# A convolution and GRU kernel: the first inputs loaded as rows and turned by TensorE, the first convolution on 32x32 tiles

## The chip, the cores and the metric

The kernel runs on one core of one Trainium2 chip. A core has five engines that run side by side and wait for one another by semaphores: TensorE (PE, matrix products, with its weight loads shown as PEld), VectorE (DVE), ScalarE (ACT), GpSimd (POOL) and SyncE (SP). 16 DMA engines move data between the chip's memory (HBM) and the core's memory (SBUF, 128 partitions); products land in PSUM. The metric is the device time of one execution in microseconds (us). The kernel before takes 1041.6 us (median of 3 runs, 1041.51 to 1042.34).

## The reference

The input x is 16 sequences of 256 steps with 512 channels, cond is 16 x 512, all in float32. First comes a causal convolution over time, separate for each channel, with 16 taps, and cond is its weights (its row k is tap k). Its result is added to x. The sum feeds a GRU cell step by step over the 256 steps, with cond as the first state too (its row b is the state of sequence b). The result is the sum plus the GRU's states.

```
x = x + conv(x, cond[:, None, :])                 # y[t] = sum_k cond[k] * x[t - 15 + k]
gi = x_t @ W_ih + b_ih ;  gh = h @ W_hh + b_hh     # 512 -> 3 x 512: r, z, n
r = sigmoid(i_r + h_r);  z = sigmoid(i_z + h_z)
n = tanh(i_n + r * h_n); h = (1 - z) * n + z * h
out = x + h
```

W_ih and W_hh are 512 x 1536, 3 MB each.

## The kernel before

**Layout.** A channel's place is (q, partition): the 512 channels lie as 4 groups q of 128 partitions, and a group's partition 32j + l is channel 128j + 32q + l. With that order a 32x32 block transpose on VectorE carries a tile with (j, sequence) on its partitions over to one with channels on its partitions. Time goes in 16 chunks of 16 steps (`CHUNKS`); a chunk's columns are 16 steps x 16 sequences = 256. `xT[c]` holds a chunk of x by channels, with a halo of 15 x 16 = 240 columns of the chunk before it; `x1T[c]` holds x plus its convolution.

**The loads.** `load_x` (L119) brings a chunk as 8 DMAs of 64 KB with rows of 512 bytes, 16 sequences by 8 steps by 128 channels each, into `x_nat`, shared out over the queues of SP, ScalarE and GpSimd for the first two chunks. cond comes in four small DMAs (L140) into `cond_nat`. `load_weights` (L171) brings a gate's weights in four DMAs (L173), on SP's queue and GpSimd's, in the order W_ih for n, W_ih for r and z, then W_hh for r, n and z, all issued in the program in front of the loop; biases are between (L158 to L163). Each queue's DMAs start in its engine's order. A DMA waits for an earlier one on the same kind of queue when its semaphore is used again, eight further on.

**The order** is written by hand: every engine executes its instructions in the order in which the program emits them (`manual_schedule`).

- `mark` and `idle_products(PAD)` (L540): four products on zeros, then 108 products of one column that compute nothing of use, and a drain, after which TensorE waits.
- `prepare_cond` (L191): VectorE turns cond to `condT` and makes `last1`, the last tap plus one (x itself is added with it).
- `turn_units(0)` (L212): VectorE turns chunk 0 in two transposes of 512 columns (L222).
- Chunk 0's convolution is split. Groups q = 0, 1 are on VectorE: one product with `last1` each (L554), then 15 taps each (L265; tap k touches 16(k+1) columns). Groups q = 2, 3 (`Q_PE`) are on TensorE: `conv_on_tensor` (L278) lets ScalarE make 32 diagonal 128x128 matrices, the identity scaled by a tap (L288), and multiplies x by each (L292), summing in PSUM; ScalarE evicts the two results (L300).
- The turns of chunk 1 (again L222) stand between VectorE's taps of chunk 0; ScalarE copies the halo (L218) and computes the first term of chunk 1's four groups (L239), between the two evictions.
- `spread_biases` (L362), seeds of the PSUM tiles by ScalarE (L371, L374), the n part of x1 @ W_ih for 8 steps (`pni`, L320, evicted at L332), the r and z part for two steps (`prz`, L383).
- `bulk.run(0, HEAD)` (L601) gives VectorE the next 27 taps of chunk 1, and step 0 five more.

**The loop** (L606) calls `step` (L403) 256 times: recurrent products for r (into `prz`), n (into `pnh`) and z on L418, 32 rows of the trace each (a float32 product is two passes), and after them, on TensorE, the input products of later steps. ScalarE and VectorE make r (L435), `rn` (L447), its transpose (L449), n (L451, tanh L459), z (L461, L465) and the new state `hist` by a scan (L474). `seen` (L398) is a one-element copy with which VectorE waits for ScalarE; step 0's stands on VectorE behind the 32 taps of chunk 1. Step 0 multiplies `condT` as the state, so it needs all of W_hh. Step 1's r products wait for step 0's `hist`.

Of the kernel before, what the change touches and what calls it, by code (L numbers as in the profile page):

```python
# [24 lines left out]
F32 = mybir.dt.float32  # L25
BF16 = mybir.dt.bfloat16
AF = mybir.ActivationFunctionType
ALU = mybir.AluOpType
PSUM = bass.MemoryType.PSUM

P = 128
L = 32
GT = 8
R, Z, N = 0, 1, 2
CHUNKS = (16,) * 16
PAD = 108
HEAD = 11.0
SYNC = mybir.DependencyInfo(mybir.DependencyClass.Sync, mybir.DependencyReason.DATA)
Q_PE = (2, 3)
NI = 8  # L40
# [35 lines left out]
def conv_gru_kernel(  # L76
# [21 lines left out]
    starts = [sum(CHUNKS[:c]) for c in range(NCH)]  # L98

    const = ctx.enter_context(tc.tile_pool(name="const", bufs=1))  # L100
# [5 lines left out]
    op = ctx.enter_context(tc.tile_pool(name="op", bufs=3))  # L106
    dram = ctx.enter_context(tc.tile_pool(name="dram", bufs=1, space=bass.MemoryType.DRAM))
    ps = ctx.enter_context(tc.tile_pool(name="ps", bufs=1, space=PSUM))
    ps_ni = ctx.enter_context(tc.tile_pool(name="ps_ni", bufs=2, space=PSUM))

    ctx.enter_context(tc.manual_schedule())

    def by_part(natural):
        return natural.rearrange("p (q l) -> p q l", q=NQ)
# [4 lines left out]
    def load_x(c, queues=((nc.sync,), (nc.sync,)), behind=None):  # L119

        n = CHUNKS[c]
        t = xin.tile([P, max(CHUNKS) // 2, P], F32, tag="x_nat", name=f"x_nat_{c}")
        for s in range(2):
            for j in range(NQ):
                made = queues[s][j % len(queues[s])].dma_start(  # L125
                    out=t[32 * j + B * s : 32 * j + B * s + B, 0 : n // 2],
                    in_=x[:, starts[c] + s : starts[c] + n : 2, j * P : (j + 1) * P],
                )
                if s == j == 0 and behind is not None:
                    tc.add_manual_dep(made.ins, behind.ins.name, SYNC, reason="later in time")  # L130
        x_nat[c] = t

    cond_nat = const.tile([P, P], F32)
    nc.vector.memset(cond_nat, 0.0)

    warm = const.tile([P, 1], F32)
    nc.vector.memset(warm, 0.0)
    blank = const.tile([P, 2 * P], BF16)
    nc.vector.memset(blank, 0.0)
    for j in range(NQ):  # L140
        (nc.sync, nc.scalar)[j % 2].dma_start(
            out=cond_nat[32 * j : 32 * j + B, :], in_=cond[:, j * P : (j + 1) * P]
        )
    load_x(0, ((nc.sync, nc.scalar), (nc.gpsimd,)))
    nc.scalar.activation(warm, warm, AF.Sigmoid)
    ident = const.tile([P, P], F32)
    make_identity(nc, ident)


    b_two = const.tile([2, 3 * C], F32)  # L150
# [3 lines left out]
    bn_nat = const.tile([P, P], F32)  # L154
    nc.vector.memset(bn_nat, 0.0)

    load_x(1, ((nc.sync,), (nc.gpsimd,)))
    nc.sync.dma_start(out=b_two[0:1, :], in_=b_hh.rearrange("(o c) -> o c", o=1))  # L158
    nc.sync.dma_start(
        out=b_two[1:2, 0 : 2 * C], in_=b_ih[0 : 2 * C].rearrange("(o c) -> o c", o=1)  # L160
    )
    nc.gpsimd.dma_start(
        out=bn_nat[0:P:L, :], in_=b_ih[2 * C : 3 * C].rearrange("(j c) -> j c", j=NQ)  # L163
    )


    wih_rz = const.tile([P, NQ, 2 * C], F32)
    wih_n = const.tile([P, NQ, C], F32)
    whh = [const.tile([P, NQ, C], F32, name=f"whh_{g}") for g in range(3)]

    def load_weights(w_sb, w, g, queues):  # L171
        for j in (0, 2, 1, 3):
            queues[j].dma_start(  # L173
                out=w_sb[L * j : L * j + L],
                in_=w[j * P : (j + 1) * P, g * C : g * C + w_sb.shape[2]].rearrange(
                    "(q l) c -> l q c", l=L
                ),
            )


    for tile_of, g in ((wih_n, N), (wih_rz, R)):
        load_weights(tile_of, w_ih, g, (nc.sync, nc.sync, nc.gpsimd, nc.gpsimd))
    zero_z = [const.tile([P, NQ * B * 2], F32, name=f"zero_z_{i}") for i in range(2)]
    for t in zero_z:
        nc.gpsimd.memset(t, 0.0)


    condT = const.tile([P, NQ, L], F32)
    last1 = const.tile([P, NQ], F32)

    def prepare_cond():  # L191
        nc.vector.transpose(condT, by_part(cond_nat))
        nc.vector.tensor_scalar_add(last1, condT[:, :, K - 1], 1.0)

    bnT = const.tile([P, NQ, L], F32)

# [3 lines left out]
    xT, x1T, ni = {}, {}, {}  # L200
# [3 lines left out]
    evictions = []  # L204
# [7 lines left out]
    def turn_units(c):  # L212

        def halo():
            xT[c] = xtp.tile([P, NQ, HALO + CMAX], F32, tag="xT", name=f"xT_{c}")
            if c:
                m = CHUNKS[c - 1] * B
                nc.scalar.copy(xT[c][:, :, 0:HALO], xT[c - 1][:, :, m : m + HALO])  # L218

        def turn(a):  # L220
            o = HALO + a * PAIR
            nc.vector.transpose(  # L222
                xT[c][:, :, o : o + GT * B].rearrange("p q (a r) -> p a q r", r=L),
                x_nat[c][:, a : a + GP].rearrange("p a (q l) -> p a q l", q=NQ),
            )
            if 2 * (a + GP) == CHUNKS[c] and 4 < c + 3 < NCH:
                load_x(c + 3)

        return [(0.0, halo)] + [
            (0.7, lambda a=a: turn(a)) for a in range(0, CHUNKS[c] // 2, GP)  # L230
        ]

    def first_terms(c):

        x1T[c] = x1p.tile([P, NQ, CMAX], F32, tag="x1T", name=f"x1T_{c}")
        n = CHUNKS[c] * B

        def first(q):
            nc.scalar.activation(  # L239
                x1T[c][:, q, 0:n],  # L240
                xT[c][:, q, HALO : HALO + n],
                AF.Copy,
                scale=last1[:, q : q + 1],
            )

        for q in range(NQ):
            firsts.append((c, q, lambda q=q: first(q)))

    def give_firsts(most=99):
        for _ in range(min(most, len(firsts))):  # L250
            firsts.pop(0)[2]()

    def lag(k):

        return (K - 1 - k) * B
# [19 lines left out]
            (0.135 + n / 960.0, lambda k=k, q=q: tap(k, q)) for k in range(K - 1) for q in range(NQ)  # L275
        ]

    def conv_on_tensor():  # L278

        n = CHUNKS[0] * B  # L280
        diag = const.tile([P, len(Q_PE), K, P], F32)

        def weight(k, q):
            return condT[:, q, k : k + 1] if k < K - 1 else last1[:, q : q + 1]

        for i, q in enumerate(Q_PE):
            for k in reversed(range(K)):
                nc.scalar.activation(diag[:, i, k], ident, AF.Copy, scale=weight(k, q))  # L288
        for i, q in enumerate(Q_PE):
            acc = ps_ni.tile([P, CHUNKS[0] * B], F32, tag="pni", name=f"conv_{q}")  # L290
            for k in reversed(range(K)):
                nc.tensor.matmul(  # L292
                    acc[:, lag(k) : n],
                    lhsT=diag[:, i, k],
                    rhs=xT[0][:, q, HALO : k * B + n],
                    start=(k == K - 1),
                    stop=(k == 0),
                    skip_group_check=True,
                )
            evictions.append(lambda q=q, acc=acc: nc.scalar.copy(x1T[0][:, q, 0:n], acc[:, 0:n]))  # L300


    blocks = [(t0, NI) for t0 in range(0, T, NI)]
# [235 lines left out]
    bulk = Plan()  # L539
    mark()  # L540
    idle_products(PAD)
    nc.tensor.drain()
    (_, halo), *turns = turn_units(0)
    halo()
    for t in hist:
        nc.vector.memset(t[:, 0:L], 0.0)
    prepare_cond()
    for _, fn in turns:
        fn()
    first_terms(0)  # L550
    firsts.clear()
    for q in range(NQ):
        if q not in Q_PE:
# [2 lines left out]
                xT[0][:, q, HALO : HALO + CHUNKS[0] * B],  # L556
                last1[:, q : q + 1],
            )
    conv_on_tensor()

    taps = [fn for i, (_, fn) in reversed(list(enumerate(tap_units(0)))) if i % NQ not in Q_PE]
    needed = (NI - 1) * (NQ - len(Q_PE))
    for fn in taps[:needed]:
        fn()
    for _, fn in turn_units(1):
        fn()
    nc.vector.transpose(bnT, by_part(bn_nat))
    for fn in taps[needed:]:
        fn()
    evictions.pop(0)()  # L570
    first_terms(1)
    give_firsts()
    evictions.pop(0)()
    spread_biases()
    nc.scalar.copy(b_rows, spare)
    seed_rz(0)
# [14 lines left out]
    for c in range(1, NCH):  # L591
        due = starts[c] - NI
        taps = tap_units(c)
# [4 lines left out]
        at = len(taps) - AHEAD  # L598
# [1 line left out]
            bulk.add(cost, due, fn)  # L600
    bulk.run(0, HEAD)  # L601

    h = (lambda kc: condT[:, kc, 0:B], condT[:, :, 0:B])
    late = []
    of_pair, of_block = [], []
    for t in range(T):  # L606
        p, s = divmod(t, 2)
# [23 lines left out]
        h = step(t, h, bulk_work, other_products)  # L631
# [41 lines left out]
```

## Time and profile before

| What | us |
|---|---|
| median of 3 runs (lowest, highest) | 1041.6 (1041.51, 1042.34) |
| the profiled execution, first to last instruction (the span) | 1039.8 |
| TensorE busy | 1022.6 (98%) |
| VectorE busy | 926.8 (89%) |
| ScalarE busy | 380.3 (37%) |
| GpSimd busy | 12.4 (1%) |
| step 1's first recurrent product starts | 36.33 |

The page prints the span alone; the profiled execution's own time has what lies around it on top, and the median run is 1.8 us above the span. In the lines of the profile, a timeline row starts with its start and its length in us, then the engine, the line of the program, the operation, the tile written and the tile read, their shapes, how many were merged into the row, and in brackets how long the engine was idle before it and what ended that. A row of the chain of waits has start, length and what the time went to; "issue" is time in which an engine waited for nothing that the profile shows. A row of the busy times by stretches has the stretch and its length, then the busy time and number of instructions of TensorE, its weight loads, VectorE, ScalarE and GpSimd, and last the granted clock, the share of the 16 DMA engines and GB/s.

### The profile page before, as it was taken

Reading aid. Unit: us, or ns where it says so; the run is one execution under the profiler, and the core shown is the slowest. Engines: PE = TensorE matmul, PEld = TensorE weight load, DVE = VectorE, ACT = ScalarE, POOL = GpSimd, SP = SyncE. Lnnn points to the kernel's source line nnn. Section 1 sums busy time; section 2 is a strip of 40 time slices with the busy share of each in tenths; the row PEclk is TensorE's granted clock in tenths of the full one; section 3 lists DMA queues with packets and bytes.
Section 4 is the critical chain, followed back from the end, with each engine's and each line's share of the span. In section 5 each row is a group of like instructions: output and inputs, shape, how many; then the busy total and the mean of one; then the engine's idle time right before and its main releaser. Section 6 shows DMA issues by size and latency. Waiting matters only on the chain.

```text
span 1039.8 us, 71852 instructions
## 1 busy us (share of the span) xinstructions
PE 1022.6 (98%) x32952; PEld 928.5 (89%) x32952; DVE 926.8 (89%) x3606; ACT 380.3 (37%) x1520; POOL 12.4 (1%) x29
## 2 busy tenths in 40 slices
PE   7899999999999999999999999999999999999997
PEld 6699999999999999999999999999999999999986
DVE  7899999999999999999999999999999999896555
ACT  6233433334333333433334333343433334333332
POOL 4000000000000000000000000000000000000000
PEclk9999999999999999999999999999999999999999
DMA  9420101101010010100100010010000000000000
GB/s 216 111 58 13 26 15 29 21 15 31 8 35 14 15 35 8 32 15 19 30 14 26 14 34 15 15 34 5 15 14 15 15 13 6 15 15 15 14 11 17
DMA packets 40850, 27.72 MB, mean 27 GB/s; under 512 B 6686, under 2 KB 38498, under 8 KB 40548
## 3 DMA queue, kind: packets, MB, share of 16 engines
q1 hardware_dynamic: 38756, 18.78, 8.0%
q8 instruction: 257, 4.21, 1.7%
q0 software_dynamic: 1376, 4.20, 1.7%
q14 instruction: 45, 0.37, 0.1%
q10 hardware_dynamic: 416, 0.16, 0.1%
HBM read 14.73 MB, written 8.39 MB: 22 GB/s over the span
## 4 chain that ended last, share of the span: by engine, by line
PE 95%; DMA 3%; DVE 1%; SPq 0%; issue 0%; ACT 0%; DVEq 0%; ACTq 0%
PE prz L418 42%; PE pnh L418 21%; PE prz L383 20%; PE pni L320 10%; DMA whh<-in_L_cond_W_hh_dram 2%; DMA x_nat<-in_x_dram 1%; DVE rnT L449 0%; DVE zp L461 0%; DVE rn L447 0%; SPq L125 0%; ACT zero_z L465 0%; DVE n L451 0%; DMA out_dram<-o 0%; DVE hist L474 0%; DVE glance L398 0%
## 5 line engine op out<-in xcount | busy, mean ns | idle before, releaser
L418 PE MATMUL prz<-whh,hist 128*32 128x128 f32 x16320 | 539.9, 273 | 3.0 <-DVE hist L474 2.1
L418 PEld LDWEIGHTS prz<-whh,hist 128*32 128x32 f32 x16320 | 450.0, 103 | 8.5 <-DVE hist L474 6.6
L265 DVE SCALAR_TENSOR_TENSOR x1T<-xT,condT,x1T 128x256 f32<-128x256 f32 (+2 forms) x930 | 377.4, 462 | 0.0
L418 PE MATMUL pnh<-whh,hist 128*32 128x128 f32 x8160 | 269.7, 273 | 0.0
L383 PE MATMUL prz<-wih_rz,x1T 128*32 128x256 f32 x4096 | 268.2, 379 | 0.1
L418 PEld LDWEIGHTS pnh<-whh,hist 128*32 128x32 f32 x8160 | 226.7, 104 | 0.0
L459 ACT ACTIVATE dn<-n 128x64 f32<-128x64 f32 x256 | 67.9, 265 | 325.9 <-DVE n L451 325.9
L383 PEld LDWEIGHTS prz<-wih_rz,x1T 128*32 128x32 f32 x4096 | 129.0, 110 | 43.7 <-issue 0.3
L320 PEld LDWEIGHTS pni<-x1T,wih_n 128*32 128x32 f32 x4096 | 122.8, 110 | 42.7 <-ACT x1T L300 0.6
L435 ACT ACTIVATE r<-prz 128x128 f32<-128x128 f32 x256 | 71.1, 278 | 238.6 <-PE prz L418 235.5
L320 PE MATMUL pni<-x1T,wih_n 128*32 128x128 f32 x4096 | 158.1, 273 | 0.0
L474 DVE TENSOR_TENSOR_SCAN hist<-zero_z,dn 128x32 f32<-128x32 f32 (+1 forms) x768 | 128.6, 216 | 0.0
L447 DVE TENSOR_TENSOR rn<-r,pnh 128x128 f32<-128x128 f32 x256 | 72.4, 283 | 38.5 <-PE pnh L418 37.2
L465 ACT ACTIVATE zero_z<-zp 128x32 f32<-128x32 f32 x512 | 90.6, 226 | 8.6 <-DVE zp L461 1.8
L449 DVE STREAM_TRANSPOSE rnT<-rn 128x128 f32<-128x128 f32 x256 | 79.7, 311 | 8.7
L461 DVE STREAM_TRANSPOSE zp<-prz 128x128 f32<-128x128 f32 x256 | 80.9, 316 | 1.8 <-PE prz L418 1.7
L332 ACT ACTIVATE ni<-pni,bnT 128x128 f32<-128x128 f32 x128 | 47.1, 368 | 74.7 <-PE pni L320 74.7
L467 DVE TENSOR_TENSOR dn<-hist,dn 128x64 f32<-128x64 f32 x255 | 58.4, 229 | 11.3
L451 DVE TENSOR_TENSOR n<-rnT,ni 128x64 f32<-128x64 f32 x256 | 57.7, 225 | 8.9
L398 DVE COPY glance<-r 1x1 f32<-1x1 f32 x256 | 34.0, 133 | 25.3 <-ACT r L435 25.3
L371 ACT COPY prz<-b_rows 128x256 f32<-128x256 f32 x128 | 48.5, 379 | 0.0
L398 DVE COPY glance<-zero_z 1x1 f32<-1x1 f32 x256 | 36.3, 142 | 8.0 <-ACT zero_z L465 0.3
(51 smaller groups left out, 211.1 us busy)
## 6 DMA issues: line engine op xcount, KB each, us to landing
out_dram<-o SPq DMA_DIRECT2D x248, 32.0 KB, 1.7
x_nat<-in_x_dram SPq DMA_DIRECT2D x118, 64.0 KB, 3.0
whh<-in_L_cond_W_hh_dram POOLq DMA_DIRECT2D x8, 256.0 KB, 14.7
wih_rz<-in_L_cond_W_ih_dram POOLq DMA_DIRECT2D x2, 512.0 KB, 10.2
wih_rz<-in_L_cond_W_ih_dram SPq DMA_DIRECT2D x2, 512.0 KB, 14.3
whh<-in_L_cond_W_hh_dram SPq DMA_DIRECT2D x4, 256.0 KB, 19.0
x_nat<-in_x_dram POOLq DMA_DIRECT2D x8, 64.0 KB, 5.4
wih_n<-in_L_cond_W_ih_dram POOLq DMA_DIRECT2D x2, 256.0 KB, 7.7
```

The source lines that it names most:

```text
L265: nc.vector.scalar_tensor_tensor(out=x1T[c][:, q, to], in0=xT[c][:, q, k * B + to.start : k * B + n], scalar=condT[:, q, k : k + 1], in1=x ...
L320: nc.tensor.matmul(hold[q][32 * j : 32 * j + 32, 0:n], lhsT=wih_n[:, kc, j * P + q * L : j * P + q * L + L], rhs=x1T[c][:, kc, o : o + n], ...
L383: nc.tensor.matmul(rz[p % 2][32 * j : 32 * j + 32], lhsT=x1T[c][:, kc, o : o + PAIR], rhs=w_rz[:, :, j * P : (j + 1) * P], start=False, st ...
L398: nc.vector.tensor_copy(glances[i][0:1], of_scalar[0:1, 0:1])
L418: product = nc.tensor.matmul(dst[32 * j : 32 * j + m], lhsT=h[0](kc), rhs=whh[g][:, kc, j * P : (j + 1) * P], start=False, stop=(kc == NQ ...
L435: of_r = nc.scalar.activation(r, pr, AF.Sigmoid)
L447: nc.vector.tensor_mul(rn, r, pnh)
L449: nc.vector.transpose(rnT, by_part(rn))
L459: nc.scalar.activation(dn_v[:, :, :, 1], n, AF.Tanh)
L461: nc.vector.transpose(zp, by_part(pz))
L465: nc.scalar.activation(z_v[:, qs, :, 1], zp[:, qs, half], AF.Sigmoid) for qs in halves
L474: nc.vector.tensor_tensor_scan(hist_g[:, lo + at : lo + end], z[:, to], dn[:, to], 0.0, op0=ALU.mult, op1=ALU.add,)
```

## The change

The first two chunks of x and cond are loaded in another shape and turned by another engine, the diagonal matrices are smaller and made by other engines, and several parts of the head stand in another order.

- `load_rows` loads half a chunk (8 steps x 16 sequences = 128 rows of 2 KB) as one DMA of 256 KB, on SP's queue or ScalarE's; four of these replace 16 loads. cond is one DMA with 16 rows of 2 KB.
- `turn_by_tensor` multiplies 16 blocks of 32 channels with an identity, which transposes them into a PSUM tile (the pool `turning` has one). VectorE copies chunk 0's two halves to `xT[0]`, ScalarE chunk 1's two to `xT[1]`. `condT` has 16 columns for each group instead of 32.
- The diagonals are 128 x 32: a 32x32 diagonal on each 32 partitions. VectorE sums the identity into this form (`ident_l`), and `make_diag` multiplies it by all taps of a group at once, on VectorE for q = 2 and on GpSimd for q = 3. `conv_on_tensor(q)` has four 32x32 products for each tap.
- The order: 72 idle products and no drain; behind them cond's turn on TensorE, then chunk 0's two halves, the convolution of q = 2, chunk 1's first half, the convolution of q = 3, chunk 1's second half. On ScalarE both evictions and then the first terms of chunk 1 follow the copies of chunk 1's halves. VectorE does all 30 taps of chunk 0 in one go. On GpSimd the diagonal and the zeroing of `zero_z` stand in front of the load of `bn_nat` and the weights. On SP the weights follow the biases as before, with two x loads in front instead of six.

```diff
-PAD = 108
+PAD = 72
+    turning = ctx.enter_context(tc.tile_pool(name="turning", bufs=1, space=PSUM))
...
+    def load_rows(c, half, queue):
+        t = const.tile([P, C], F32, name=f"x_rows_{c}_{half}")
+        t0 = starts[c] + half * GT
+        queue.dma_start(
+            out=t, in_=x[:, t0 : t0 + GT, :].rearrange("b t c -> t b c")
+        )
+        x_rows[c, half] = t
...
-    load_x(0, ((nc.sync, nc.scalar), (nc.gpsimd,)))
+    nc.scalar.dma_start(out=cond_nat, in_=cond)
+    for c in range(2):
+        for half in range(2):
+            load_rows(c, half, (nc.sync, nc.scalar)[half])
...
+    nc.vector.tensor_reduce(
+        out=ident_l,
+        in_=ident.rearrange("p (i l) -> p l i", l=L),
+        op=ALU.add,
+        axis=mybir.AxisListType.X,
+    )
...
-    load_x(1, ((nc.sync,), (nc.gpsimd,)))
...
+    def turn_by_tensor(turned, rows, unit):
+        for q in range(NQ):
+            for j in range(NQ):
+                at = j * P + q * L
+                nc.tensor.matmul(
+                    turned[L * j : L * j + L, q],
+                    lhsT=rows[:, at : at + L],
+                    rhs=unit,
+                    start=q == 0,
+                    stop=q == NQ - 1,
+                    skip_group_check=True,
+                )
...
-        nc.vector.transpose(condT, by_part(cond_nat))
+        turned = turning.tile([P, NQ, K], F32, tag="turned", name="cond_turned")
+        turn_by_tensor(turned, cond_nat, ident[0:B, 0:B])
+        nc.vector.tensor_copy(condT, turned)
...
+    def turn_rows(c, half, engine):
+        turned = turning.tile([P, NQ, P], F32, tag="turned", name=f"x_turned_{c}_{half}")
+        turn_by_tensor(turned, x_rows[c, half], ident)
+        to = xT[c][:, :, HALO + half * P : HALO + half * P + P]
+        if engine is nc.scalar:
+            nc.scalar.copy(to, turned)
+        else:
+            engine.tensor_copy(to, turned)
...
+    def make_diag(engine, q):
+        diag[q] = const.tile([P, K, L], F32, name=f"diag_{q}")
+        parts = ((slice(0, K - 1), condT[:, q, 0 : K - 1]), (slice(K - 1, K), last1[:, q : q + 1]))
+        for to, w in parts:
+            n = to.stop - to.start
+            engine.tensor_tensor(
+                out=diag[q][:, to],
+                in0=ident_l.unsqueeze(1).broadcast_to([P, n, L]),
+                in1=w.unsqueeze(2).broadcast_to([P, n, L]),
+                op=ALU.mult,
+            )
...
-        for i, q in enumerate(Q_PE):
-            for k in reversed(range(K)):
-                nc.scalar.activation(diag[:, i, k], ident, AF.Copy, scale=weight(k, q))
...
+        for k in reversed(range(K)):
+            for j in range(NQ):
+                rows = slice(L * j, L * j + L)
                 nc.tensor.matmul(
-                    acc[:, lag(k) : n],
-                    lhsT=diag[:, i, k],
-                    rhs=xT[0][:, q, HALO : k * B + n],
+                    acc[rows, lag(k) : n],
+                    lhsT=diag[q][rows, k],
+                    rhs=xT[0][rows, q, HALO : k * B + n],
...
-    nc.tensor.drain()
...
     prepare_cond()
-    for _, fn in turns:
-        fn()
+    make_diag(nc.vector, Q_PE[0])
+    for q in Q_PE[1:]:
+        make_diag(nc.gpsimd, q)
+    nc.gpsimd.dma_start(
+        out=bn_nat[0:P:L, :], in_=b_ih[2 * C : 3 * C].rearrange("(j c) -> j c", j=NQ)
+    )
+    for tile_of, g in ((wih_n, N), (wih_rz, R)):
+        load_weights(tile_of, w_ih, g, (nc.sync, nc.sync, nc.gpsimd, nc.gpsimd))
+    turn_units(0)[0][1]()
+    turn_rows(0, 0, nc.vector)
+    turn_rows(0, 1, nc.vector)
...
-    conv_on_tensor()
+    conv_on_tensor(Q_PE[0])
+    turn_units(1)[0][1]()
+    turn_rows(1, 0, nc.scalar)
+    for q in Q_PE[1:]:
+        if len(evictions) > 1:
+            evictions.pop(0)()
+        conv_on_tensor(q)
+        if q == Q_PE[1]:
+            turn_rows(1, 1, nc.scalar)
...
-    evictions.pop(0)()
     first_terms(1)
+    while evictions:
+        evictions.pop(0)()
     give_firsts()
-    evictions.pop(0)()
...
-    h = (lambda kc: condT[:, kc, 0:B], condT[:, :, 0:B])
+    h = (lambda kc: condT[:, kc], condT)
```

More of the change, by code (lines that the diff above doesn't have):

```diff
@@ L131, in load_x @@
         x_nat[c] = t
-    cond_nat = const.tile([P, P], F32)
-    nc.vector.memset(cond_nat, 0.0)
+    def load_rows(c, half, queue):
[5 more added lines that the diff above has]
+        x_rows[c, half] = t
+    x_rows = {}
+    cond_nat = const.tile([B, C], F32)
     warm = const.tile([P, 1], F32)
@@ L139, in conv_gru_kernel @@
     nc.vector.memset(blank, 0.0)
[L140 to L143, printed above, removed]
-    load_x(0, ((nc.sync, nc.scalar), (nc.gpsimd,)))
+    nc.scalar.dma_start(out=cond_nat, in_=cond)
+    for c in range(2):
+        for half in range(2):
+            load_rows(c, half, (nc.sync, nc.scalar)[half])
     nc.scalar.activation(warm, warm, AF.Sigmoid)
@@ L147, in conv_gru_kernel @@
     make_identity(nc, ident)
+    ident_l = const.tile([P, L], F32)
+    nc.vector.tensor_reduce(
[4 more added lines that the diff above has]
+    )
     b_two = const.tile([2, 3 * C], F32)
@@ L160, in conv_gru_kernel @@
         out=b_two[1:2, 0 : 2 * C], in_=b_ih[0 : 2 * C].rearrange("(o c) -> o c", o=1)
-    )
-    nc.gpsimd.dma_start(
-        out=bn_nat[0:P:L, :], in_=b_ih[2 * C : 3 * C].rearrange("(j c) -> j c", j=NQ)
     )
@@ L178, in load_weights @@
             )
-    for tile_of, g in ((wih_n, N), (wih_rz, R)):
-        load_weights(tile_of, w_ih, g, (nc.sync, nc.sync, nc.gpsimd, nc.gpsimd))
     zero_z = [const.tile([P, NQ * B * 2], F32, name=f"zero_z_{i}") for i in range(2)]
@@ L185, in conv_gru_kernel @@
         nc.gpsimd.memset(t, 0.0)
-    condT = const.tile([P, NQ, L], F32)
+    condT = const.tile([P, NQ, K], F32)
     last1 = const.tile([P, NQ], F32)
+    def turn_by_tensor(turned, rows, unit):
[10 more added lines that the diff above has]
+                )
     def prepare_cond():
-        nc.vector.transpose(condT, by_part(cond_nat))
+        turned = turning.tile([P, NQ, K], F32, tag="turned", name="cond_turned")
+        turn_by_tensor(turned, cond_nat, ident[0:B, 0:B])
+        nc.vector.tensor_copy(condT, turned)
         nc.vector.tensor_scalar_add(last1, condT[:, :, K - 1], 1.0)
+    def turn_rows(c, half, engine):
[6 more added lines that the diff above has]
+            engine.tensor_copy(to, turned)
     bnT = const.tile([P, NQ, L], F32)
@@ L276, in tap_units, with conv_on_tensor @@
         ]
-    def conv_on_tensor():
-        n = CHUNKS[0] * B
-        diag = const.tile([P, len(Q_PE), K, P], F32)
-        def weight(k, q):
-            return condT[:, q, k : k + 1] if k < K - 1 else last1[:, q : q + 1]
-        for i, q in enumerate(Q_PE):
-            for k in reversed(range(K)):
-                nc.scalar.activation(diag[:, i, k], ident, AF.Copy, scale=weight(k, q))
-        for i, q in enumerate(Q_PE):
-            acc = ps_ni.tile([P, CHUNKS[0] * B], F32, tag="pni", name=f"conv_{q}")
-            for k in reversed(range(K)):
+    diag = {}
+    def make_diag(engine, q):
[9 more added lines that the diff above has]
+            )
+    def conv_on_tensor(q):
+        n = CHUNKS[0] * B
+        acc = ps_ni.tile([P, CHUNKS[0] * B], F32, tag="pni", name=f"conv_{q}")
+        for k in reversed(range(K)):
+            for j in range(NQ):
+                rows = slice(L * j, L * j + L)
                 nc.tensor.matmul(
-                    acc[:, lag(k) : n],
-                    lhsT=diag[:, i, k],
-                    rhs=xT[0][:, q, HALO : k * B + n],
+                    acc[rows, lag(k) : n],
+                    lhsT=diag[q][rows, k],
+                    rhs=xT[0][rows, q, HALO : k * B + n],
                     start=(k == K - 1),
@@ L299, in conv_on_tensor @@
                 )
-            evictions.append(lambda q=q, acc=acc: nc.scalar.copy(x1T[0][:, q, 0:n], acc[:, 0:n]))
+        evictions.append(lambda: nc.scalar.copy(x1T[0][:, q, 0:n], acc[:, 0:n]))
     blocks = [(t0, NI) for t0 in range(0, T, NI)]
@@ L541, in conv_gru_kernel @@
     idle_products(PAD)
-    nc.tensor.drain()
-    (_, halo), *turns = turn_units(0)
-    halo()
     for t in hist:
@@ L558, in conv_gru_kernel @@
             )
-    conv_on_tensor()
+    conv_on_tensor(Q_PE[0])
[7 more added lines that the diff above has]
+            turn_rows(1, 1, nc.scalar)
     taps = [fn for i, (_, fn) in reversed(list(enumerate(tap_units(0)))) if i % NQ not in Q_PE]
[L562 to L565, printed above, removed]
+    for fn in taps:
         fn()
     nc.vector.transpose(bnT, by_part(bn_nat))
-    for fn in taps[needed:]:
-        fn()
-    evictions.pop(0)()
     first_terms(1)
+    while evictions:
+        evictions.pop(0)()
     give_firsts()
-    evictions.pop(0)()
     spread_biases()
```

## The prediction

> **What bounds the kernel now.** I read the page first (busy shares), then the chain that ended last in order of time for the first 60 us, then the timeline of each engine over the same stretch, then busy time by stretches of 4 us. The page says that TensorE is the bound of the whole, and the chain says that it is not so at the start:
>
> ```profile
> PE 1022.6 (98%) x32952; PEld 928.5 (89%) x32952; DVE 926.8 (89%) x3606; ACT 380.3 (37%) x1520; POOL 12.4 (1%) x29
> ...
> q8 instruction: 257, 4.21, 1.7%
> ```
>
> ```profile
> 11.42 22.65 DMA whh<-in_L_cond_W_hh_dram
> 34.07 0.14 issue
> 34.20 1.10 PE prz L418 x32
> ...
> 36.33 1.08 PE prz L418 x32
> 37.42 0.87 PE pnh L418 x32
> 38.29 0.87 PE prz L418 x32
> ```
>
> From 36.33 us, where step 1's first products (R) begin, TensorE runs without a gap to the end: 1039.8 - 36.33 = 1003.5 us that the change does not touch (the order and shapes of all instructions are the same from step 0's first recurrent product on). Only the head can move. In the head the last weight load lands at 34.07 and step 1 follows 2.26 us later. Close behind it is a second bound, VectorE:
>
> ```profile
> 9.26 0.62 DVE L554 TENSOR_SCALAR x1T<-xT,last 128x256 f32<-128x256 f32 x2
> 9.91 4.70 DVE L265 SCALAR_TENSOR_TENSOR x1T<-xT,condT,x1T 128x240 f32<-128x240 f32 x14
> 14.53 1.30 DVE L222 STREAM_TRANSPOSE xT<-x_nat 128x512 f32<-128x512 f32 x2
> 15.75 0.27 DVE L567 STREAM_TRANSPOSE bnT<-bn_nat 128x128 f32<-128x128 f32 x1
> 15.94 15.99 DVE L265 SCALAR_TENSOR_TENSOR x1T<-xT,condT,x1T 128x128 f32<-128x128 f32 x48
> 31.85 0.13 DVE L398 COPY glance<-r 1x1 f32<-1x1 f32 x1
> ```
>
> All 32 taps of chunk 1 that stand in front of step 0's glance are in that last row (16 small ones of chunk 0 come first, 3.24 us; chunk 1 begins at 19.18 and takes 32 x 0.396 = 12.67 us). In the loop R follows 1.8 us after rn, so VectorE's end plus 1.87 us is the earliest step 1: 33.8 now, hidden by the weights.
>
> Two more rows matter. TensorE ran at half pace until about 13.5 us (14 matmul records in 4 us, then 31), though the granted clock (third column from the end) reads 1.00; and it stood still 1.14 us with its weights landed and nothing to wait for:
>
> ```profile
> 10.00:14.00 4.00, 4.00 (x14) 3.69 (x13) 4.00 (x13) 4.00 (x14) 3.01 (x7) 1.00 1.05 219
> 14.00:18.00 4.00, 4.00 (x31) 3.92 (x30) 4.00 (x15) 2.49 (x6) 1.10 (x2) 1.00 1.03 292
> ```
>
> ```profile
> 27.95 0.38 PE L418 MATMUL prz<-whh,condT 128*16 128x128 f32 x2 [0.77 <-DMA whh<-in_L_cond_W_hh_dram]
> 29.46 0.95 PE L418 MATMUL prz<-whh,condT 128*16 128x128 f32 x27 [1.14 <-issue]
> ```
>
> The queue q8 of the page moves 257 packets of 16 KB; TensorE has 65,925 records, 256 to a packet: it is TensorE's code. By the single packet records, a packet starts in the loop when TensorE passes record 193 + 256n (within 0.4 us), and in the head, where the 16 DMA engines are full (share 1.0 from 3 to 32.5 us), late:
>
> ```
> boundary, reached us    193, 4.40   449, 22.22   705, 29.46   961, 36.33   1217, 40.31
> packet starts us          6.69        26.56        32.42        36.03        40.03
> lag us                    2.3         4.3          3.0          -0.3         -0.3
> ```
>
> The halt from 28.06 to 29.46 lies exactly at record 705, 2.9 us after the packet of 26.56 started. I read it so: passing boundary n orders the block behind boundary n+1, which is usable 2.9 us after its packet starts. In the loop (256 records in 3.94 us) that fits; under full DMA it takes 2.3 to 4.3 + 2.9 = 5.2 to 7.2 us a block.
>
> **The change part by part.** *x and cond as rows, turned by TensorE.* Gone: 16 x loads, 4 cond loads, four 128x512 transposes (2 x 1.30 us) and the cond transpose (0.31). The two transposes of chunk 1 leave VectorE's busy stretch (-1.3). New before the convolution: 36 fewer idle products (x 0.028, they end near 3.8), cond's 16 products of 16 columns (32 records; 0.3 to 0.9 us, between the quick issue of L362 and 0.028 each, + 0.27 to finish), a copy (0.2): x's first half can begin at 4.6 to 5.3. Its rows must have landed: the first x loads of 64 KB landed at 4.13 to 4.68 now; 256 KB each, issued 1 us earlier, I put at 4 to 5.6. A half is 32 records of 128 columns: 1.07 us at full clock (row 34.20), about 1.9 at half pace; then a 512-column copy from PSUM, no such row, 0.65 by the transposes of that size (0.69) and 0.48 for 384 columns on ScalarE. The one PSUM tile makes the halves strictly serial: 2 x (1.07 to 1.9 + 0.65 + 0.12) = 3.7 to 5.3. So x is ready at 8.3 to 10.6; I take 10.0 against 9.23 now, as the idle products did not bring full clock before 13.5 in this trace.
>
> *Queues.* SP loses 6 x and 2 cond issues, but b_two's load waits for a memset that now stands behind the reduction, which waits for GpSimd's identity (about 1.9): 3.5 instead of 2.7, and SP's weights queue behind it, from 4.1 instead of 6.89. GpSimd loses 8 issues x 0.53 and gets a diagonal of 512 columns (0.29 for 128 columns of the affine select: about 1.2), waiting for cond; its weight issues start near 7 instead of 6.71 and no longer wait for slots (last issue near 13.5, not 21.28). x in 2 KB rows: mean packet 140 ns against 4 x 42 for 512 B, so 0 to 3 us saved on 30. Z's weights land at 30 to 33.9, step 1 not before 32.3 to 36.2 on their account. Below the sum, so I cost it at nothing; its cover is the chain that follows.
>
> *Diagonals.* ScalarE loses 32 x 0.292 = 9.3 us; VectorE's 512-column diagonal (0.7 by 0.225 for 64 columns) and the reduction lie before x is ready. Nothing either way. The halo copy (0.98) moves in front of the evictions on ScalarE, which is idle then.
>
> *Convolution on 32x32 tiles, 128 matmuls instead of 32.* Columns per block: 16 + 32 + ... + 256 = 2176, two passes; four tiles side by side at L383's pace (256 columns, four tiles, 0.215 us) give 3.75 us, against 4.4 now at full clock. No row shows tiles with different input rows side by side; serial would be 14.6. I take 3.75: four column tiles do run together in L418, L383 and L320. About 1.0 us is added for the half-pace start (0 to 2).
>
> [...]
>
> *The new wait.* ScalarE's first terms of chunk 1 now stand behind both turned halves and both evictions, and the last half (x_turned_1_1) is on TensorE behind the second convolution. VectorE reaches chunk 1 at 10.0 + 0.65 + 4.62 + 3.24 + 0.25 = 18.8 and then waits for them. Call E the end of that last turn. Then copy 0.52, two evictions 0.6, first term 0.5, waits 0.1: taps begin at E + 1.72, take 12.67, and step 1 follows at +1.87, that is E + 16.3.
>
> Without code stalls E = 10.0 + 0.14 + 3.75 + 1.0 + 0.87 + 3.75 + 1.1 + 0.6 (four changes of tile form, 0.15 each by the gap before L362) = 21.2: step 1 at 37.5, +1.2.
>
> *Code.* In the changed program the first convolution starts at record 350, the second at 671, the last turn at 928 to 991 (now: 229 and 293). Boundary 449 lies 6 taps into the first convolution, at 10.0 + 0.14 + 2.16 + 0.9 = 13.2. The block from 705 is then usable at 13.2 + 3.3 + 2.9 = 19.4, while TensorE wants it at about 17.4. The block from 961, in the middle of the last turn, follows at 19.4 + 6.2 = 25.6, wanted at 23.0. E = 25.6 + 0.7 = 26.3, step 1 at 42.6: +6.2 us. With lags of 2.3 and 4.3 and x ready at 9 to 10.6 it is +3.6 to +8.8. The rest of TensorE's head (biases, pni, prz, N, Z) ends before VectorE's 40.7.
>
> [...]
>
> **Sum.** Span 1039.8 + 6.2 = 1046.0; the median run, 1041.6, is 1.8 above the profiled span: 1047.8.
>
> **The rivals.** *No code stall* (the 26.56 packet was late for some other reason): 1042.8, 1040.5 to 1045 with x ready at 8.3 to 10.6 and the slow clock 0 to 2 us. For it: the loop shows none. Against: the halt sits on the boundary. *Tiles serial*: +21.7 on E without stalls, 1064 to 1069; for it, no row shows the form; against, column tiles overlap. *Faster*: VectorE is not held up, because tiles overlap more than column tiles do (1.9 us a convolution), full clock comes by 5 us, and code is there: x ready 8.3, chunk 1 from 17.1, step 1 at 31.6 or, if later, weights + 2.26, 32.3 to 34: 1037.6 to 1039.3. It decides once E is under 18.0. Against it: L418 and L383 both keep 0.84 ns a column.
>
> **How the numbers follow.** Code-bound 0.60 (1045.2 to 1050.4); no code stall 0.24; serial tiles 0.07; faster 0.09, of which a third stays within 0.2%. 0.2% is 2.1 us, about what a measurement of this kernel can tell from no change. Of the no-stall case a quarter lies above 1043.7. Slower 0.60 + 0.06 + 0.07 = 0.73, same 0.18 + 0.03 = 0.21, faster 0.06. The range leaves out serial tiles, the upper tail and most of the faster case: 1040.5 to 1050.5.
>
> **What would show it.** Right: halts of TensorE without a releaser at records 705 and 961, VectorE waiting some 9 us for ScalarE before chunk 1, step 1's R released by VectorE near 42. Wrong: the last turn ends before 22, or step 1 is still released by a weight load.

## The result and the profile after

The changed kernel takes 1051.9 us (median of 4 runs, 1050.4 to 1053.0) against 1042.0 us for the kernel before on the same chip (1041.51 to 1043.93): 1.0088 times as long, 95% interval [1.0066, 1.0110]. The profiled execution took 1052.3 us, 0.3 above the median, with a span of 1050.4 us against 1039.8: 10.6 us more.

The page first, with its row of the code queue and a group of instructions (behind the bar: busy time, mean ns, and the idle time in front with its releaser). TensorE is still busy 98% of the span; VectorE's taps have 11.5 us of idle time in front of them, ended by ScalarE's first terms.

```profile
q8 instruction: 260, 4.26, 1.8%
...
L301 DVE SCALAR_TENSOR_TENSOR x1T<-xT,condT,x1T 128x256 f32<-128x256 f32 (+2 forms) x930 | 377.3, 462 | 11.5 <-ACT x1T L275 11.5
```

The chain of waits of the changed kernel (start, length, what) shows the whole head on one path. Up to 29.45 us it is TensorE's, with two standstills called "issue"; then ScalarE's copies, VectorE's 32 taps, and step 1's first products (R) at 45.58:

```profile
18.19 1.14 PE conv L336 x17
19.33 1.42 issue
20.75 3.09 PE conv L336 x97
23.84 0.66 PE x_turned L206 x17
24.50 4.27 issue
28.77 0.68 PE x_turned L206 x15
...
31.05 12.76 DVE x1T L301 x32
...
45.58 1.08 PE prz L462 x32
46.66 1.50 PE pnh L462 x32
48.16 1.71 PE prz L462 x32
```

The two standstills lie in the middle of the second convolution and in the middle of the last turn (`x_turned_1_1`), where the program has nothing to wait for. By count they are TensorE's records 705 and 961. Step 1 starts 9.25 us later than before. The last two lines are the rest: N and Z of step 1 took 1.50 and 1.71 us, and 0.87 each in the kernel before. The stretches of 4 us show why: the granted clock (third column from the end) is low behind the standstills.

```profile
30.00:34.00 4.00, 3.86 (x76) 2.89 (x76) 2.95 (x8) 3.97 (x13) 0.00 (x0) 0.61 1.05 216
...
46.00:50.00 4.00, 4.00 (x93) 3.73 (x88) 2.74 (x10) 0.71 (x3) 0.00 (x0) 0.59 0.02 4
```

From step 1 to the end the kernels are alike. Span less the start of step 1 is 1003.5 us before and 1004.8 after; the two slow products, 1.47 us longer together, cover these 1.3 us.

### The profile page after: what moved, and what is told of

It is laid out like the page before. It is cut to its first block, busy times and chain, and to the rows that moved or that the text cites. A ratio compares the mean times of both kernels' runs of the same rounds, so it can differ in the third digit from the quotient of the medians.

```text
span 1050.4 us, 72425 instructions
## 1 busy us (share of the span) xinstructions
PE 1030.4 (98%) x33268; PEld 930.8 (89%) x33268; DVE 927.8 (88%) x3606; ACT 372.0 (35%) x1490; POOL 9.8 (1%) x23
## 4 chain that ended last, share of the span: by engine, by line
PE 95%; DVE 2%; issue 1%; DMA 1%; ACT 0%
PE prz L462 42%; PE pnh L462 21%; PE prz L427 20%; PE pni L364 10%; DVE x1T L301 1%; PE conv L336 1%; PE x_turned L206 1%; DMA x_rows<-in_x_dram 0%; DVE rnT L493 0%; DVE rn L491 0%; DMA out_dram<-o 0%; DVE zp L505 0%; ACT zero_z L509 0%; DVE n L495 0%; DVE xT L229 0%
## 5 line engine op out<-in xcount | busy, mean ns | idle before, releaser
L301 DVE SCALAR_TENSOR_TENSOR x1T<-xT,condT,x1T 128x256 f32<-128x256 f32 (+2 forms) x930 | 377.3, 462 | 11.5 <-ACT x1T L275 11.5
L491 DVE TENSOR_TENSOR rn<-r,pnh 128x128 f32<-128x128 f32 x256 | 72.3, 282 | 38.5 <-PE pnh L462 37.2
```

The lines of the kernel that those rows point to most:

```text
L301: nc.vector.scalar_tensor_tensor(out=x1T[c][:, q, to], in0=xT[c][:, q, k * B + to.start : k * B + n], scalar=condT[:, q, k : k + 1], in1=x ...
L491: nc.vector.tensor_mul(rn, r, pnh)
```

## The experiments

Theory A: TensorE's code comes in blocks of 256 records (260 packets on q8, 66,560 records of TensorE in the changed kernel), and while the DMA engines are full (share 0.99 to 1.09 in every 2 us from 10 to 34 us in the changed kernel) a block comes so late that TensorE halts at its first record (1.42 us at 705, 4.27 at 961); the change puts more records in front of step 1 (1596 instead of 961), so more such halts. The rivals are named at each experiment. All times are from the profiles, and ratios are to runs of the kernel before on the same chip.

### Without the weights' transfers

```
 def load_weights(w_sb, w, g, queues):
-    for j in (0, 2, 1, 3):
-        queues[j].dma_start(out=w_sb[L * j : L * j + L], in_=w[...])
+    nc.gpsimd.memset(w_sb, 0.0)
```

> The changed kernel without its weight loads: GpSimd fills the weights with zeros (6 MB of transfers are left out, so the output is not the reference's); TensorE's instructions are the same. Theory A (a block of code that starts late because the DMA engines are full halts TensorE): the halts at records 705 and 961 (1.42 and 4.27 us in the changed kernel) are gone, the last turn ends near 23.8 us instead of 29.45, step 1 starts near 40 (that end + 16.1), the time falls to 1045 to 1047. Rival B (TensorE halts at these places whatever the DMA engines do): the halts stay, step 1 near 45.6, time 1051 to 1053.

Measured: 1047.7 us, ratio 1.0053 [1.0037, 1.0069]. The timeline of TensorE (start, length, instruction) has no standstill in the convolutions and the last turn:

```profile
16.74 3.93 PE L330 MATMUL conv<-xT,diag 32*32 32x256 f32 x128
...
20.60 1.08 PE L200 MATMUL x_turned<-ident,x_rows 128*32 128x128 f32 x32
```

The code packets behind the boundaries at 449 and 705 started at 13.16 and 17.15, TensorE passed the boundaries at 14.10 and 17.42: no lag, as in the loop. The share of the DMA engines was 0.05 or less from 8 to 23 us here, and 1.00 to 1.08 in the changed kernel. So the halts come from the weights' transfers, and B falls. The last turn ended at 21.7 (I had said 23.8). But step 1 started only at 40.65, and the time lies above the 1045 to 1047 us that I had said, for a reason that the experiment brought with it: while GpSimd filled the weights (7.10 to 17.6), VectorE's two scalings, 0.72 us together in the changed kernel, took 7.53, and its taps started 6.7 us later than there.

```profile
10.50 7.53 DVE x1T L598 x2
...
18.05 7.97 DVE x1T L295 x30
```

So it shows where the halts come from, and not what they cost.

### The last turn ahead of the second convolution

```
     turn_rows(1, 0, nc.scalar)
+    turn_rows(1, 1, nc.scalar)
     for q in Q_PE[1:]: ...
-        if q == Q_PE[1]:
-            turn_rows(1, 1, nc.scalar)
...
     first_terms(1)
+    give_firsts()
     while evictions:
         evictions.pop(0)()
-    give_firsts()
```

> The changed kernel with the last turn ahead of the second convolution, and ScalarE's first terms of chunk 1 ahead of its two evictions. Same instructions, same records. Theory A (code bounds TensorE up to step 0's Z products as well, not only the last turn): the last turn ends near 21.5, VectorE is done near 35.5 instead of 43.8, but the code of step 0's products comes no earlier, Z still ends near 43.1 and step 1 starts near 44.2: time 1049 to 1051. Rival C (VectorE's late start is the whole loss): step 1 at the last weight's landing, 38.7, + 2.26 = 41.0: time 1046 to 1047.5.

Measured: 1051.1 us, ratio 1.0082 [1.0067, 1.0097], the same as the changed kernel. The last turn ended at 22.1, VectorE was free, and step 1 started at 46.29, later than the 45.58 of the changed kernel, with the weights landed by 39.05. In the chain of this run VectorE's taps are gone, and TensorE's halts are still there:

```profile
25.87 3.72 issue
...
36.87 1.78 issue
38.65 0.95 PE pni L364 x25
...
46.29 1.08 PE prz L462 x32
```

Rival C (VectorE's late start is the whole loss) falls. Two paths of about the same length end at step 1: the last turn with VectorE's taps behind it, and TensorE's own work up to Z, which waits for the blocks from records 961 and 1217. Both are set by the code. I had said 44.2 for step 1; the block from record 1217 came at 38.65, 2.2 us later than in the changed kernel.

### Half of the change at a time

The first kernel has rows and turns as in the change, and the convolution as before on 128x128 diagonals (384 records fewer). The second is the kernel before with the 32x32 convolution (384 records more).

```
-            for j in range(NQ):
-                rows = slice(L * j, L * j + L)
-                nc.tensor.matmul(acc[rows, lag(k) : n], lhsT=diag[q][rows, k], ...)
+            nc.tensor.matmul(acc[:, lag(k) : n], lhsT=diag[:, Q_PE.index(q), k], ...)
```

> Half of the change alone: rows turned by TensorE, with the convolution as before (32 products on 128x128 diagonals by ScalarE; 384 records fewer). Theory A: the last turn ends at record 606, ahead of boundary 705, so no halt lies before it: it ends near 23.6 and VectorE is no longer last; the weights are (38.7 + 2.26 = 41.0): time 1045.5 to 1048. Rival B (the halts belong to the places, not to the count of records): the last turn ends near 29, time 1051 to 1053.

> The other half alone: the kernel before with the convolution on 32x32 diagonals, made by VectorE and GpSimd (384 records more ahead of step 1). Theory A: halts at records 705, 961 and 1217, each some 7 us after the one before, Z ends near 36 and step 1 starts at 37 to 38.5 instead of 36.33: time 1042.5 to 1044.5. Rival D (only the loads and turns cost): the weights still come last, 1041 to 1042.

Measured: 1045.0 us, ratio 1.0026 [1.0017, 1.0036], and 1043.8 us, ratio 1.0010 [1.0000, 1.0020]. With the rows alone nothing halts before the last turn ends at 23.4, and VectorE's taps behind it set step 1 to 39.54 (the weights, which I had named, had landed by 35.07). The time is just under what I had said (1045.5). With the 32x32 convolution alone the halts are where the count puts them: 705 is near the end of the second convolution, and 961 is among the input products, which are the same as in the kernel before. Step 1 starts at 38.83 us, so rival D falls:

```profile
18.35 2.81 issue
21.15 0.34 PE conv L307 x15
...
26.81 2.58 issue
...
38.83 1.08 PE prz L433 x32
```

The third, at 1217, did not come: there was no standstill when TensorE passed it at 35.67. The first half costs some 2.5 us at the medians, the second some 1.2 (its interval reaches down to no change), and together they cost 9.9: only together do two halts fall ahead of the end of the turn that VectorE waits for.

### The pause in front of step 1

```
         first = recurrent(pz, Z)
+        if t == 0:
+            for _ in range(18):
+                nc.tensor.matmul(spare[:, 0:2], lhsT=blank[:, 0:P], rhs=blank, ...)
```

> The changed kernel with 18 idle products (bf16, 256 columns) between step 0's Z products and step 1's R products, where TensorE stands still for 2.52 us in the changed kernel. Theory E (a pause of that length brings TensorE back to half pace: step 1's R, N and Z products took 1.08, 1.50 and 1.71 us instead of 1.08, 0.87 and 0.87): they return to 0.9 to 1.1 each, time 1049.8 to 1050.8 against 1051.9 of the changed kernel. Rival (the slow products are late code or a late releaser): no change, 1051.5 to 1052.5.

Measured: 1050.9 us, ratio 1.0066 [1.0049, 1.0083]. The interval overlaps that of the changed kernel, so the time alone does not show it; the profile does. Step 1 started at 45.84 and its products were back at full pace. In the traces' clock records the granted clock is 0.50 from 46.74 to 50.16 us in the changed kernel, and here it stays at 1.00 from 35.25 us on to the end of the loop:

```profile
46.92 0.87 PE pnh L462 x32
47.80 0.87 PE prz L462 x32
```

Span less step 1 is 1003.2 us in this run. It is 1003.1 to 1003.6 in every run here whose pause ahead of step 1 was 1.9 us or less, and 1004.8, 1004.8 and 1005.8 after pauses of 2.52 (the changed kernel), 6.29 (no weights' transfers) and 3.88 us (the next run).

### The loads on 16 DMA engines

```
     queue.dma_start(
-        out=t, in_=x[:, t0 : t0 + GT, :].rearrange("b t c -> t b c")
+        out=t, in_=x[:, t0 : t0 + GT, :]
     )
...
-    turn_by_tensor(turned, x_rows[c, half], ident)
+    turn_by_tensor(turned, x_rows[c, half], unit_bt)   # unit matrix, columns by (t, b)
```

> The changed kernel with each half chunk's rows laid on the partitions by sequence and then by step (TensorE turns them with a permuted unit matrix), so that the load runs over 16 sequences at its slowest and is shared by 16 DMA engines, not 8 as in the changed kernel. Theory A: the last weight lands 2 to 5 us earlier than 38.7, but the weights do not end last; the halts stay: 1050 to 1052. Rival F (the load on 8 engines holds up the head): the last turn ends 3 us or more earlier, time under 1048.5.

Measured: 1052.2 us, ratio 1.0079 [1.0063, 1.0094]. The loads' semaphores got 8 counts from the engines in the changed kernel and 16 here. From 2 to 5 us the share of the 16 DMA engines was 0.43 in the changed kernel, and 0.93 in the kernel with both turns first (below), which loads x as this one does. The last weight landed at 33.94 us instead of 38.70. The time did not move, since the halts stayed (20.31 and 28.34 us are their ends), and F falls.

### The place of the halts, and the queue

The first kernel starts with 40 idle products instead of 72, the second has all 20 weight loads on SP's queue, the third starts with no idle products.

```
-PAD = 72
+PAD = 40        # in the third: PAD = 0
...
-    load_weights(tile_of, w_ih, g, (nc.sync, nc.sync, nc.gpsimd, nc.gpsimd))
+    load_weights(tile_of, w_ih, g, (nc.sync, nc.sync, nc.sync, nc.sync))   # the second; W_hh too
```

> The changed kernel with 40 idle products instead of 72 at the start: every later record comes 64 records sooner in the count, nothing else moves (TensorE waits for cond and x behind them). Theory A: halts stay at records 705 and 961 by count, which are now 32 products later in the program: the first further into the second convolution, the second behind the last turn. The last turn ends at 25.5 to 27 instead of 29.45; Z still waits for the code from 1217, so step 1 starts at 42 to 45.5: 1048 to 1052. Rival B (halts belong to places of the program): they stay 17 products into the second convolution and 17 into the last turn, which ends at 28.5 to 29.5.

> The changed kernel with all 20 weight loads on SP's queue (12 of them were on GpSimd's). It asks what makes a block of code late: in the changed kernel the packets started 3.3 us (record 449) and 5.2 us (record 705) after TensorE had passed the boundary before. Theory H (the code packet waits its turn among the queues that have packets ready): with one queue of weights in place of two the 5.2 us fall under 3.5, the last turn ends near 27 or earlier, time 1046 to 1050. Rival I (it waits for DMA engines that are full, whoever fills them): 4.5 to 6 us again, the last turn ends near 29, time 1050.5 to 1053, later if the weights on one queue land after 42.

> The changed kernel with the 72 idle products taken out and nothing else: 144 records fewer in front of everything (boundary 705 moves to the end of the second convolution, 961 behind the last turn, into the input products). Theory A, with TensorE at full pace from about 10 us as in the version with the turns first and no idle products: the last turn ends at 21 to 23.5 instead of 29.45, Z waits for the blocks from 961 and 1217 (8 us each) and ends near 39 to 41, step 1 starts at 40 to 42.5 instead of 45.6, without the half pace that followed: 1045 to 1048. Rival C (the last turn alone sets the end): step 1 at 38 to 39, 1043 to 1044.5.

Measured: 1049.3 us, ratio 1.0056 [1.0039, 1.0074]; 1048.6 us, ratio 1.0050 [1.0030, 1.0069]; 1050.2 us, ratio 1.0073 [1.0060, 1.0086]. With 40 idle products the halts moved with the count: the first comes after 49 products of the second convolution instead of 17, the second behind the last turn, which ended at 27.2 (I said 25.5 to 27; TensorE ran at half pace after the halt: the turn's 32 records took 1.91 us, and 1.08 in the run without the weights' transfers). Rival B falls a second time:

```profile
17.63 2.44 PE conv L336 x49
20.07 3.21 issue
...
25.31 1.91 PE x_turned L206 x32
```

With no idle products they moved to records 449, 705 and 961 at 16.43, 22.62 and 32.35, the last turn ended at 28.2, and step 1 started at 45.18: outside what I expected (40 to 42.5). The full pace that I had counted on from 10 us came at 14.5 there, and behind the second halt the granted clock was 0.50 from 24.75 to 38.40 us, in which the last turn and most of the input products ran.

With one queue of weights the first block's packet started at 14.11, 0.9 us ahead of TensorE at the boundary, and the halt at 705 was gone. The second started 4.8 us late, the third 5.9. The stretches show a difference: the share of the DMA engines (second column from the end) was lower around the first than around the others.

```profile
14.00:16.00 2.00, 2.00 (x56) 1.50 (x49) 2.00 (x8) 0.00 (x0) 0.00 (x0) 1.00 0.85 188
...
22.00:24.00 2.00, 0.26 (x9) 0.00 (x0) 0.00 (x0) 0.00 (x0) 0.00 (x0) 1.00 1.03 224
```

By the lags H (the number of queues) falls: with one queue of weights two packets were still 4.8 and 5.9 us late, where H had them under 3.5. But the time and the end of the last turn (27.1) came out as H had said, because the first halt was gone, and not as I (full DMA engines) had said, 1050.5 to 1053 us. I fits the two stretches; it is not shown, since in the microsecond around the first packet's start (13.5 to 14.5 us) the share was still 0.95.

From the single packet records, eight of the standstills; over all of them in these runs the last column lies between 2.4 and 3.0 us:

```
run                  record   packet starts   TensorE goes on   us between
changed                 705           17.98             20.75         2.77
changed                 961           25.94             28.77         2.83
changed                1217           33.73             36.46         2.73
last turn first         961           26.76             29.59         2.83
32x32 in before         705           18.58             21.15         2.57
40 idle products        961           29.19             31.82         2.63
no idle products        449           15.23             17.91         2.68
one queue               961           23.16             26.00         2.84
```

### Both turns first, and the convolution as before

Both turns of chunk 1 stand ahead of the second convolution, the loads are on 16 engines, the convolution is as before on 128x128 diagonals, and ScalarE's first terms come ahead of its evictions. The first kernel has 72 idle products, the second none.

> Rows turned by TensorE and loaded on 16 DMA engines, the convolution as before on 128x128 diagonals, both turns of chunk 1 ahead of the second convolution, ScalarE's first terms of chunk 1 ahead of its evictions. Theory A: VectorE is done near 33 (37.8 with the turns as they were), the weights land by 35, and the code of record 961, in step 0's first products, comes near 33.5, so Z ends near 37 and step 1 starts at 37.5 to 38.5 (39.5): 1043 to 1045. Rival C (only VectorE's chain counts): step 1 at 35 to 36.5: 1040.3 to 1042.

> The version with both turns first and the convolution on 128x128 diagonals, without the 72 idle products at the start: 1069 records ahead of step 1 instead of 1213. Theory A: boundary 961 moves from R's products to the end of N's, its code comes near 35 (33.48 in the version before), with only some 108 records to go behind it instead of 252, so step 1 starts at 37 to 38.5 (40.3), and the time is 1040.5 to 1042, at or just under the kernel before (1041.2 to 1045.8 in these comparisons). Rival B (the halt belongs to the place): it stays 4 products into R and step 1 at 40: 1043 to 1044. Rival J (the idle products bring TensorE's full pace forward, so without them the convolution is slower): the second convolution ends later than 24.1 by 1 us or more, 1043 or more.

Measured: 1043.5 us, ratio 1.0002 [0.9992, 1.0012], and 1041.3 us (median of 12 runs, the kernel before 1042.7 beside it), ratio 0.9982 [0.9972, 0.9993]. In the first, step 0's first products halt after 4 of them, at record 961, and step 1 starts at 40.30, 1.8 us later than I said (the packet's lag was 5.2 us, and TensorE ran at half pace behind the halt: 13 records of `prz` on the input took 1.50 us, 16 of them 0.86 in the loop). But this execution, 1045.4 us, is the slowest of the 12, 1.9 us above the median; with that taken off, step 1 of a median run starts near 38.4, by estimate, which is what I had said (37.5 to 38.5):

```profile
30.62 2.87 issue
...
40.30 1.08 PE prz L458 x32
```

In the second the same boundary falls into N's products, where TensorE has just waited for a weight anyway. The halt is 0.70 us, and step 1 starts at 35.47 (I had said 37 to 38.5), against 36.33 in the kernel before:

```profile
15.87 15.29 DMA whh<-in_L_cond_W_hh_dram
...
32.00 0.70 issue
...
35.47 1.08 PE prz L458 x32
```

Rival J (slower convolutions without idle products) falls: the first took 4.63 us instead of 6.36, and the second ended at 21.7 instead of 24.1. So this kernel differs from the one with 72 idle products in its faster start too, and not only in where the boundaries fall. The gain over the kernel before is small, about 1.4 us at the medians, and at the edge of what can be told apart. That the missing idle products alone are not the gain shows the last run, the kernel before without its 108:

> The kernel before without its 108 idle products and nothing else. It asks whether these alone are what the best version gains. Theory A: step 1 still waits for the last weight (34.07 + 2.26), and the code of record 705, now 40 records ahead of step 1, comes at 33 to 35: step 1 at 36 to 37, time within 0.15% of the kernel before. Rival K (the idle products cost the kernel before its time): step 1 at 35.5 or earlier, 0.15% or more faster.

Measured: 1042.6 us, ratio 0.9999 [0.9987, 1.0012]. K falls. In the profiled execution (1043.7 us, 1.2 above the median) the last weight landed at 35.90 us and step 1 started at 38.53, later than the 36 to 37 that I had said.

## Why the prediction was wrong

The direction and the mechanism were right; the size was not: 1047.8 us (1040.5 to 1050.5) was said, 1051.9 measured. Its own steps, in us of the span:

```
step                                     said              measured
x ready for the convolution              10.0              10.57
boundary 449 reached                     13.2              14.9
its packet, and the use of it            3.3 + 2.9         3.0 + 2.8
record 705 wanted, usable                17.4, 19.4        19.3, 20.75
from there to record 961 usable          3.3 + 2.9 = 6.2   5.2 + 2.8 = 8.0
record 961 wanted, usable                23.0, 25.6        24.5, 28.77
E, end of the last turn                  26.3              29.45
from E to step 1                         16.3              16.13
step 1                                   42.6              45.58
span less step 1                         1003.5            1004.8
```

- **The mis-sized term is the second block's lag.** I put one lag, 3.3 us, on both packets, while the table of the kernel before had 2.3, 4.3 and 3.0. The packet for 961 took 5.2 us from the moment that TensorE could pass 705 to its start. That is 1.8 us of the 4.4 by which the span was missed. In the later runs whose weights were still landing, that packet was 4.3 to 5.9 us late, whichever way the loads were arranged; why it is later than the first stays open.
- **The start of it: 1.35 us.** x was ready 0.6 us later, and half pace lasted to 16.0 us (there the trace's clock records begin, and the second convolution is faster than the first), where I had allowed 1.0 us for it; the first convolution took 6.57 us instead of 4.75.
- **A term was left out: 1.3 us.** A pause of 2.52 us in front of step 1 cost half pace behind it (granted clock 0.50 from 46.74 to 50.16 us). I had priced half pace for the start of the kernel only. With the two terms above, less the 0.2 us by which the chain from E to step 1 was shorter than said, that makes up the 4.4 us. In these runs a pause of 2.52 us was followed by half pace, and pauses of up to 1.9 us were not.
- **"The rest of TensorE's head ends before VectorE's 40.7" failed.** Z ended at 43.06, since it waits for record 1217's code (halt to 36.46). It cost nothing beside VectorE's 43.8, but the run with the turn first showed that it would have been next, and no cheaper.
- **The halts were as described**: without a releaser, at records 705 and 961, ended 2.8 us after their packets started. VectorE stood still for 11.5 us (some 9 said), and the chain from E to step 1 was within 0.2 us. In the loop the packets of the kernel before start from 0.8 us ahead of the boundary to 0.8 behind it, not within 0.4; nothing rests on that.
- **No code stall** fell with the first run, where the halts went with the transfers. In the loop of the changed kernel the crossing of a block costs nothing that the profile shows (from 50 us on TensorE's waits come to 1.0 us, for `hist`), and in its head one crossing cost 4.27 us.
- **Tiles serial** fell: with no halt inside (the run with one queue of weights), the second convolution's 127 records of products took 3.86 us, where 3.75 was said (the row it was taken from, 0.215 us for 256 columns, gives 3.66):

```profile
17.74 3.86 PE conv L336 x127
```

By the row of 0.215 us (0.84 ns a column) one tile after the other would have taken 14.6 us, by estimate. The four tiles of a tap write to one PSUM tile, each to its own 32 partitions, and they did run together.
- **Faster** needed an E under 18.0; even without the weights' transfers it was 21.7.
- **The weights' cover was thinner than I said.** I put their last landing at 30 to 33.9 us; it was 38.70. With the x loads on 16 engines it was 33.94. And I had read that GpSimd's weight issues "no longer wait for slots", with the last issue near 13.5 us: that was wrong. Five of them waited for earlier loads of that queue to land, and the load that landed last was issued at 28.03:

```profile
28.03 0.55 POOL L185 DMA_DIRECT2D whh<-in_L_cond_W_hh_dram  x1 [2.48 <-DMA wih_rz<-in_L_cond_W_ih_dram]
```

It stayed hidden.
- **The low end of the code-bound range** was added up wrongly: with x ready at 9 us and lags of 2.3 the terms give +3.3 us, not +3.6. Nothing rests on it.

## What to carry to other kernels

Count instructions, not only their time, in a head in which the DMA engines are full: where one halt followed another, the blocks of 256 TensorE records came 7.4 to 9.1 us apart, against the 3.94 us in which TensorE used one up in the loop, so a form that computes the same in more and smaller products can lose although each is as cheap as was hoped. When a halt has no releaser, count its records: if its place follows the count, shift or shorten the code; 144 records less went with some 2 us in one kernel (ratio 1.0002 to 0.9982, with a faster start beside it) and with nothing clear in another (1.0088 to 1.0073). And look for the second path before buying off the first: here two ended within 1 us of each other.

## What the runs showed that I had not expected

- A fill by GpSimd slowed VectorE: two scalings that take 0.72 us together took 7.53 while GpSimd filled the weight tiles, and ended 0.4 us after the last fill.
- TensorE fell back to half pace after a pause of 2.52 us, and it came to full pace at the start at very different times: at 8.4 us in the fastest version, 13.6 in the kernel before and 16.0 in the changed one. The traces' clock records begin at these moments, so in the stretches before them the granted clock reads 1.00 all the same, while later, from 30 to 34 and from 46 to 50 us, the half pace shows as 0.61 and 0.59. What sets the moment stays open: leaving out the idle products went with an earlier one in the fastest version and not in the kernel before.
- Half pace came behind the halts too: in the changed kernel the granted clock was 0.50 from 29.67 to 33.09 us, behind the halt that ended at 28.77. That stretch and the one behind the pause in front of step 1 are 3.41 us long each; in the changed kernel without idle products one was 13.65 us long, four times as much.
- Why a packet of code starts 3 us late once and 5 another time (7.3 us for the first one with 40 idle products), with the DMA engines about equally full (shares of 1.06, 1.09 and 1.05 in the 2 us in which the three packets of the changed kernel started, 3.0, 5.2 and 5.0 us late), stays open too; one queue of weights in place of two did not end it.
